# Silu by tanh, the norms' reciprocal root as a power on GpSimd: one ScalarE table per layer

## The chip, the cores and the metric

The kernel runs on one core of a Trainium2 chip. The metric is device time in microseconds. The profile is one execution of the program, taken by the hardware profiler. Engines in it: PE is TensorE, PEld its weight loads, DVE is VectorE, ACT is ScalarE, POOL is GpSimd, SP is SyncE, which here only issues DMAs.

## What is computed

Two layers of the same frame over x of 32 sequences of 256 rows of 128, that is 8192 rows:

```python
xn = _layernorm(x)                       # (x - mean) / sqrt(var + eps)
x = x + attn0(xn) * silu(ffn0(xn))       # layer 0
xn = _layernorm(x)
x = x + attn1(xn) * silu(ffn1(xn))       # layer 1
```

`attn0` is a causal attention of 16 heads of 8 whose pattern is a product of two score matrices, without a softmax. `ffn0` is a mixture of eight experts with gelu and two experts to a row, plus a shared expert; its output is divided by the largest absolute value of its row. `attn1` is a softmax attention over a strided and local set of keys. `ffn1` is a mixture of eight experts with relu, two to a row and a fixed capacity.

## The kernel before

The unit of work is a pair of sequences: `TT` = 4 tiles of 128 rows, so there are `NP` = 16 pairs. In the order of time:

- `begin` (L286), for each pair: `layernorm` (L116), a transpose and the router's product. Beside it the first steps of layer 0's attention run. `route0` (L303) then picks two experts for each row and gives each row a slot.
- Rows are scattered to their slots in device memory by indirect DMAs on POOL (L158), while the attention goes on; then the experts run (`experts`, L572), fetching weights and rows, with some attention steps between.
- The combine of layer 0, `combine0` (L614), for each pair, beside the rest of the attention. It gathers eight tiles of expert rows by indirect DMAs on POOL (L623, into `rows`, four buffers), sums them with their gates on DVE (L632), takes the row's maximum (L636 to L638), applies silu on ACT (L641), multiplies by the attention's output on POOL (L642), adds to x on DVE (L643), writes x back, and takes layer 1's norm (L646), whose result PE transposes for the next router (L650).
- Layer 1: `route1`, a first half of the attention (pairs 0 to 7) while POOL scatters rows, the experts with all weights resident (L1001 to L1044), then the second half of the attention (pairs 8 to 15) beside `combine` (L1050), which gathers expert rows (L1055), sums them with their gates (L1067, L1068), applies silu (L1070), multiplies (L1073), adds (L1074) and stores.

Layer 0's attention handles a sequence in 8 steps. A step transposes features (`ptr`, L440), copies them out of PSUM on ACT (`qk`, L442), makes four pattern matmuls (`pp`, L457) and multiplies them by the causal mask on DVE (`pat`, L459). There are 256 of these products in the run, so they count the attention's progress. Layer 1's attention works in stacks of 128 queries: scores (L831, L838), row maximum and difference on DVE (L846, L847), exponential on ACT (L848), transposes on PE (L853), a copy on ACT (L855), the product with the values (L862).

`layernorm` takes mean and variance on DVE (L121, L122), the root of the variance plus eps on ACT (L124), its reciprocal on DVE (L126), the shift `lnnb` on DVE (L128), and scales four tiles on ACT (L130).

Three things set the order. Each engine works off its own queue in order, so an instruction that waits holds what stands behind it. The order within the queues is made by a scheduler when the program is built, from the order in which the generators above are stepped; PE's order in layer 1's attention is fixed by hand. The generators are stepped by two plans. In layer 0 a pair is started every six attention steps, and its six parts follow at these offsets:

```python
EVERY, LATER = 6, (0, 6, 7, 8, 11, 13)
t0 = at
plan = sorted((t0 + EVERY * p + d, p, n) for p in range(NP) for n, d in enumerate(LATER))
```

In layer 1 the three parts of `combine` come at stacks 2, 5, 6 of every four for the later pairs and 0, 3, 3 for the earlier ones (L1082 to L1087). And the helper `pace` (L138) lets indirect DMAs go three at a time: after every third, a small memset (`breath`, L142) on POOL waits until the three have landed.

ACT evaluates its functions from tables. In the profile a table load (ACT_TABLE_LOAD) stands in front of an activation whose table is not the one that was loaded last: in front of Sqrt, Silu, Gelu, Exp and Sigmoid when the function before was another of these. No load stands in front of copies or of Identity.

Of the kernel before, what the change touches and what calls it, by code (L numbers as in the profile page):

```python
# [11 lines left out]
F32 = mybir.dt.float32  # L12
BF16 = mybir.dt.bfloat16
I32 = mybir.dt.int32
AF = mybir.ActivationFunctionType
ALU = mybir.AluOpType
# [4 lines left out]
P = 128  # L21
# [8 lines left out]
TT = PT // P  # L30
# [5 lines left out]
EPS = 1e-5  # L36
# [6 lines left out]
def bc(ap, axis, n):  # L43

    ap = ap.unsqueeze(axis)
    shape = list(ap.shape)
    shape[axis] = n
    return ap.to_broadcast(shape)
# [8 lines left out]
def model_kernel(ctx: ExitStack, tc: tile.TileContext, a: dict, out: bass.AP):  # L57
    nc = tc.nc
# [12 lines left out]
    const = ctx.enter_context(tc.tile_pool(name="const", bufs=1))  # L71
# [13 lines left out]
    make_identity(nc, ident)  # L85
    identb = const.tile([P, P], BF16, name="identb")
    nc.vector.tensor_copy(identb, ident)
    eps = const.tile([P, 1], F32, name="eps")
    nc.gpsimd.memset(eps, EPS)
    riota = const.tile([P, E], F32, name="riota")  # L90
    nc.gpsimd.iota(riota, [[-1, E]], base=E, channel_multiplier=0,
                   allow_small_or_imprecise_dtypes=True)
# [23 lines left out]
    def layernorm(pool, src, dst, n):  # L116

        st = pool.tile([P, n, 6], F32, tag="lnst", name="lnst")
        mv = pool.tile([P, n, 2], F32, tag="lnmv", name="lnmv")
        for i in range(n):  # L120
            nc.vector.bn_stats(st[:, i, :], src[:, i, :])  # L121
            nc.vector.bn_aggr(mv[:, i, :], st[:, i, :])  # L122
        sd = pool.tile([P, n], F32, tag="lnsd", name="lnsd")
        nc.scalar.activation(sd, mv[:, :, 1], AF.Sqrt, bias=eps)  # L124
        rs = pool.tile([P, n], F32, tag="lnrs", name="lnrs")
        nc.vector.reciprocal(rs, sd)  # L126
        nb = pool.tile([P, n], F32, tag="lnnb", name="lnnb")
        nc.vector.scalar_tensor_tensor(nb, mv[:, :, 0], -1.0, rs, ALU.mult, ALU.mult)  # L128
        for i in range(n):
            nc.scalar.activation(dst[:, i, :], src[:, i, :], AF.Identity, bias=nb[:, i : i + 1],  # L130
                                 scale=rs[:, i : i + 1])
# [89 lines left out]
    with ExitStack() as c0:  # L221
# [26 lines left out]
        def load(p):  # L248
            x = wk.tile([P, TT, P], F32, tag="x", name="x", bufs=6)
            nc.sync.dma_start(x, xin[:, p * TT : (p + 1) * TT, :])  # L250
            return x
# [31 lines left out]
        def mm_tile(name):  # L283
            return ps_m.tile([P, 512], F32, tag="mm", name=name)
# [329 lines left out]
        def combine0(p):  # L614

            t = slice(p * TT, (p + 1) * TT)
            x = load(p)
            so = bk.tile([P, 2, TT, P], F32, tag="soin", name="soin")
            nc.sync.dma_start(so, part[p])
            rows = bk.tile([P, 2, TT, P], F32, tag="rows", name="rows")  # L620
            for i in range(TT):
                for k in range(2):
                    pace(lambda: nc.gpsimd.indirect_dma_start(  # L623
                        out=rows[:, k, i, :], out_offset=None, in_=moe0[:, :],
                        in_offset=bass.IndirectOffsetOnAxis(
                            ap=slot0[:, k, p * TT + i : p * TT + i + 1], axis=0),
                    ))
            yield
            acc = so[:, 1]
            for i in range(TT):  # L630
                for k in range(2):
                    nc.vector.scalar_tensor_tensor(acc[:, i, :], rows[:, k, i, :],  # L632
                                                   gate0[:, k, p * TT + i : p * TT + i + 1],
                                                   acc[:, i, :], ALU.mult, ALU.add)
            mx = wk.tile([P, TT], F32, tag="mx", name="mx")
            nc.vector.tensor_reduce(mx, acc, AX.X, ALU.max, apply_absolute_value=True)  # L636
            nc.vector.tensor_scalar(mx, mx, 1e-6, None, ALU.add)
            nc.vector.reciprocal(mx, mx)  # L638
            yield
            for i in range(TT):  # L640
                nc.scalar.activation(acc[:, i, :], acc[:, i, :], AF.Silu, scale=mx[:, i : i + 1])  # L641
            nc.gpsimd.tensor_tensor(acc, acc, so[:, 0], ALU.mult)  # L642
            nc.vector.tensor_tensor(x, x, acc, ALU.add)  # L643
            nc.sync.dma_start(x1[p], x)
            yield
            layernorm(wk, x, xn[:, t, :], TT)  # L646
            yield
            pst1 = mm_tile("pst1")
            for i in range(TT):
                nc.tensor.transpose(pst1[:, i * P : (i + 1) * P], xn[:, p * TT + i, :], ident)  # L650
            xnT1 = wk.tile([P, PT], F32, tag="xnT1", name="xnT1")
            nc.scalar.copy(xnT1, pst1)
            yield
            psl = mm_tile("psl")
            pl = psl[:, : TT * E].rearrange("p (i e) -> p i e", e=E)
            for i in range(TT):
                nc.tensor.matmul(pl[:, i, :], lhsT=xnT1[:, i * P : (i + 1) * P], rhs=wg1,
                                 start=True, stop=True)
            nc.vector.tensor_copy(logit[:, t, :], pl)
            yield  # L660
# [65 lines left out]
        while plan or at < NP * SPP:  # L726
# [7 lines left out]
            while plan and plan[0][0] < now and plan[0][1] <= (now - 4) // SPP - 1:  # L734
                _, p, n = plan.pop(0)
# [194 lines left out]
    def route1(pool):  # L930
        with ExitStack() as cr:
            rp = cr.enter_context(tc.tile_pool(name="rp", bufs=1))
            NK2 = 2 * NT
            (m0, r0, oh0), (_, r1, oh1) = top2(rp, logit, NT)
            rs = rp.tile([P, 2, NT], F32, name="rs")
            for k, r in enumerate((r0, r1)):
                nc.vector.tensor_copy(rs[:, k, :], r)
            ohf, _, pos = counted(rp, pool, "h", oh0, oh1)
            own = rp.tile([P, E, NK2], F32, name="own")
            for i in range(2):  # L940
                nc.vector.tensor_tensor(own[:, 4 * i : 4 * i + 4, :], pos[i][:, :, :NK2],
                                        ohf[:, 4 * i : 4 * i + 4, :], ALU.mult)
            loc = rp.tile([P, 2, NT], F32, name="loc")
            locf = loc.rearrange("p k n -> p (k n)")
            nc.vector.tensor_reduce(locf, own.rearrange("p e n -> p n e"), AX.X, ALU.add)

            valid = rp.tile([P, 2, NT], F32, name="valid")
            nc.vector.tensor_scalar(valid, loc, float(CAP), None, ALU.is_le)

            slot = rp.tile([P, 2, NT], F32, name="slot")  # L950
            nc.vector.tensor_scalar(slot, rs, -float(CAP), float(E * CAP - 1), ALU.mult, ALU.add)
            nc.vector.tensor_scalar(loc, loc, float(CAP), None, ALU.min)
            nc.vector.tensor_tensor(slot, slot, loc, ALU.add)
            nc.vector.tensor_copy(gidx, slot)
            drop = rp.tile([P, 2, NT], F32, name="drop")
            nc.vector.tensor_scalar(drop, valid, -SKIP, SKIP, ALU.mult, ALU.add)
            nc.vector.tensor_tensor(slot, slot, drop, ALU.add)
            nc.vector.tensor_copy(sidx, slot)  # L958


            ex = rp.tile([P, NT, E], F32, name="ex")
            nc.vector.tensor_tensor(ex, logit, bc(m0, 2, E), ALU.subtract)
            nc.scalar.activation(ex, ex, AF.Exp)
            z = rp.tile([P, NT], F32, name="z")
            nc.vector.tensor_reduce(z, ex, AX.X, ALU.add)
            nc.vector.reciprocal(z, z)
            nc.vector.tensor_tensor(ex, ex, bc(z, 2, E), ALU.mult)
            for k, oh in enumerate((oh0, oh1)):
                nc.vector.tensor_tensor(oh, oh, ex, ALU.mult)
                nc.vector.tensor_reduce(gate[:, k, :], oh, AX.X, ALU.add)  # L970
            nc.vector.tensor_tensor(z, gate[:, 0, :], gate[:, 1, :], ALU.add)
            nc.vector.reciprocal(z, z)
            nc.vector.tensor_tensor(gate, gate, bc(z, 1, 2), ALU.mult)
            nc.vector.tensor_tensor(gate, gate, valid, ALU.mult)

# [21 lines left out]
    with ExitStack() as cm:  # L997
# [35 lines left out]
        rows = [(e, e * CAP + q * MT) for e in range(E) for q in range(CAP // MT)]  # L1033
# [13 lines left out]
    with ExitStack() as cb:  # L1047
        bk = cb.enter_context(tc.tile_pool(name="bk", bufs=3))

        def combine(p):  # L1050

            rows = bk.tile([P, 2, TT, P], F32, tag="rows", name="rows")
# [11 lines left out]
            y = bk.tile([P, TT, P], F32, tag="yc", name="yc")  # L1064
            for i in range(TT):
                n = p * TT + i
                nc.vector.tensor_scalar(y[:, i, :], rows[:, 0, i, :], gate[:, 0, n : n + 1], None, ALU.mult)  # L1067
                nc.vector.scalar_tensor_tensor(y[:, i, :], rows[:, 1, i, :], gate[:, 1, n : n + 1],  # L1068
                                               y[:, i, :], ALU.mult, ALU.add)
            nc.scalar.activation(y, y, AF.Silu)  # L1070
            yield
            s = att.late[p] if p >= NEARLY else sres[:, p * TT : (p + 1) * TT, :]
            nc.vector.tensor_tensor(y, y, s, ALU.mult)  # L1073
            nc.vector.tensor_tensor(y, y, x, ALU.add)  # L1074
            nc.sync.dma_start(outv[:, p * TT : (p + 1) * TT, :], y)
# [122 lines left out]
```

## Time and profile before

| what | value |
|---|---|
| three runs | 2206.1, 2211.04, 2212.84 us; median 2211.04 us |
| profiled execution | 2215.44 us, of which the span is 2213.7 us |
| granted TensorE clock, mean of the span | 0.928 of full speed |
| DVE, waiting for POOL at L643 | 90.5 us, 11 times |
| table loads on ACT | 86, each 1.283 us |
| POOL product L642, 128x512 | 16, mean 1.329 us |
| POOL tensor_tensor L422, 128x1024 | 16, mean 1.954 us |
| DVE 128x512 products (L643, L1073, L1074) | mean 0.66 to 0.69 us |
| silu L641, 128x128 with a scale per row | 64, mean 0.401 us |
| silu L1070, 128x512 | 16, mean 0.630 us |
| root L124, 128x4 | 32, mean 0.301 us |

Stages by the timeline: first norms and routing to about 180 us, scatter to 450, experts to 850, combine of layer 0 with the rest of its attention to 1258, routing and first attention of layer 1 to 1573, its experts to 1819, second attention and combine to the end.

How the page is read: a row of groups gives line, engine, operation, what is written and read, shapes, count, then busy time and the mean in ns of one, then the idle time of the engine just before them and who ended it. A row of waits says which engine at which line waited for whom, how long in total, how often, and the longest. A row of the timeline starts with the start and the length in us; in brackets stands the idle time of the engine before it and what ended it. The clock row and the granted clock say how fast TensorE was allowed to run.

### The profile page before, as it was taken

To read this page: it belongs to the slowest core of one execution; us is meant where nothing else is said; L and a number is where in the kernel's file an instruction comes from. 1 tells how busy PE (TensorE), PEld (TensorE's weight loads), DVE (VectorE), ACT (ScalarE), POOL (GpSimd) and SP (SyncE) were. 2 spreads that over 40 slices of the span, in tenths; PEclk is the share of its full clock that TensorE was granted. 3 is DMA by queue.
4 is the path that set the end of the run, shared out by engine and by line. 5 is a ranking of instruction groups with operands and counts; after the bars stand their busy time and mean duration, and the time that the engine had idled before them with its cause. 6 is when DMAs were issued, how large, how long until landed. Compare 5 with 4: busy or idle time off the path is not lost.

```text
span 2213.7 us, 45584 instructions
## 1 busy us (share of the span) xinstructions
PE 1963.4 (89%) x18674; PEld 1445.9 (65%) x18674; DVE 1232.4 (56%) x2609; ACT 968.0 (44%) x1977; POOL 662.9 (30%) x817
## 2 busy tenths in 40 slices
PE   6999999799999998765969589999999995789898
PEld 4777677588888886544747466666677773456565
DVE  5666766432222224554768477777433335677776
ACT  5623333233334433434746346566311114565655
POOL 0004555413223222555530045543000004444300
PEclk9989999899999999877979789999999997788889
DMA  8702111145545443222220311110122211212100
GB/s 256 215 1 68 52 45 35 57 123 156 156 147 174 147 149 110 77 80 67 82 69 35 110 32 35 38 34 23 53 69 71 72 61 52 52 49 62 44 25 11
DMA packets 131457, 176.80 MB, mean 80 GB/s; under 512 B 16305, under 2 KB 94660, under 8 KB 131249
## 3 DMA queue, kind: packets, MB, share of 16 engines
q1 hardware_dynamic: 103056, 96.57, 13.6%
q0 software_dynamic: 26752, 76.03, 11.7%
q8 instruction: 148, 2.42, 0.5%
q10 hardware_dynamic: 1440, 1.27, 0.2%
q14 instruction: 61, 0.49, 0.1%
HBM read 104.78 MB, written 69.21 MB: 79 GB/s over the span
## 4 chain that ended last, share of the span: by engine, by line
PE 40%; DMA 5%; POOL 4%; ACT 3%; issue 3%; DVE 1%; POOLq 0%; ACTq 0%; DVEq 0%; SPq 0%
PE apsT L853 6%; PE apav L862 6%; PE mpsd L1027 5%; PE mpsu L1014 5%; PE apsc L838 3%; DMA rows<-moe,slot 3%; PE apsc L831 3%; POOL rows L623 2%; DMA rows<-moe,gidx 2%; PE apsf L873 1%; PE apsv L815 1%; ACT apr L848 1%; PE apsk L803 1%; POOL rows L1055 1%; PE pp L457 1%
## 5 line engine op out<-in xcount | busy, mean ns | idle before, releaser
L457 PE MATMUL pp<-qk 64*128 64x128 f32 x2048 | 209.7, 308 | 105.7 <-DVE pat L459 55.5
L442 ACT COPY qk<-ptr 128x512 f32<-128x512 f32 x256 | 149.1, 585 | 353.0 <-PE y L469 270.4
L457 PEld LDWEIGHTS pp<-qk 64*128 64x128 f32 x2048 | 148.0, 192 | 177.2 <-issue 129.8
L459 DVE TENSOR_TENSOR pat<-pp,dmask 128x512 f32<-128x512 f32 x256 | 175.2, 684 | 129.3 <-PE pp L457 128.4
L855 ACT COPY apT<-apsT 124x512 f32<-124x512 f32 x256 | 146.9, 585 | 217.9 <-PE apsT L853 216.6
L1055 POOL DMA_INDIRECT rows<-moe,gidx x128 | 124.5, 973 | 338.8 <-ACT aqT L800 286.5
L862 PEld LDWEIGHTS apav<-ava,apT 124*64 124x64 f32 x4096 | 143.6, 140 | 113.5 <-issue 52.9
L158 POOL DMA_INDIRECT disp<-xn,slot x128 | 136.4, 1066 | 222.4 <-DVE state L432 173.0
L846 DVE TENSOR_REDUCE amx<-apsc 128x4 f32<-128x496 f32 x256 | 159.8, 665 | 75.3 <-PE apsc L838 74.8
L853 PE MATMUL apsT<-ident,apr 128*124 128x128 f32 x1024 | 170.5, 301 | 29.4 <-ACT apT L855 14.6
L608 DVE TENSOR_TENSOR od<-edn,wt 128x256 f32<-128x256 f32 x72 | 30.5, 424 | 287.5 <-PE edn L604 287.5
L862 PE MATMUL apav<-ava,apT 124*64 124x9 f32 x4096 | 167.0, 208 | 22.8 <-ACT apT L855 21.7
L597 ACT ACTIVATE ha<-eup,wt 128x256 f32<-128x256 f32 x288 | 119.0, 470 | 129.7 <-PE eup L592 126.8
L440 PE MATMUL ptr<-ident,feat 128*128 128x128 f32 x1024 | 171.5, 286 | 0.9 <-DVE feat L422 0.6
L848 ACT ACTIVATE apr<-apr 128x496 f32<-128x496 f32 x256 | 149.5, 618 | 30.0 <-DVE apr L847 29.8
L847 DVE TENSOR_TENSOR apr<-apsc,amx 128x496 f32<-128x496 f32 x256 | 159.1, 662 | 0.0
L563 POOL DMA_INDIRECT wt<-in_wexp,wrow x72 | 69.0, 959 | 297.0 <-DVE xdT L585 264.2
L623 POOL DMA_INDIRECT rows<-moe,slot x128 | 133.0, 1039 | 65.6 <-issue 29.0
L853 PEld LDWEIGHTS apsT<-ident,apr 128*124 128x124 f32 x1024 | 120.3, 149 | 47.5 <-ACT apT L855 19.7
L158 POOL DMA_INDIRECT disp<-xn,sidx x128 | 125.8, 983 | 80.5 <-DVE sidx L958 27.1
L440 PEld LDWEIGHTS ptr<-ident,feat 128*128 128x128 f32 x1024 | 120.7, 146 | 43.4 <-issue 38.0
L592 PE MATMUL eup<-xdT,wt 128*128 128x256 f32 x576 | 142.3, 389 | 1.8 <-DMA wt<-in_wexp,wrow 1.8
(217 smaller groups left out, 3671.6 us busy)
## 6 DMA issues: line engine op xcount, KB each, us to landing
disp<-zero SPq DMA_DIRECT2D x17, 1024.0 KB, 6.9
xd<-disp SPq DMA_DIRECT2D x72, 128.0 KB, 2.0
moe<-od SPq DMA_DIRECT2D x72, 128.0 KB, 2.0
x<-in_x SPq DMA_DIRECT2D x32, 256.0 KB, 3.2
part<-so SPq DMA_DIRECT2D x16, 512.0 KB, 3.1
soin<-part SPq DMA_DIRECT2D x16, 512.0 KB, 3.7
xd<-disp SPq DMA_DIRECT2D x32, 256.0 KB, 2.6
moe<-od SPq DMA_DIRECT2D x32, 256.0 KB, 2.0
```

The costliest lines, as they stand in the source:

```text
L158: ins = pace(lambda: nc.gpsimd.indirect_dma_start(out=self.dst[:, :], out_offset=bass.IndirectOffsetOnAxis(ap=idx, axis=0), in_=rows, in_o ...
L440: nc.tensor.transpose(pst[:, 2 * n + c], seq.feat[c][:, n, m * P : (m + 1) * P], ident)
L442: nc.scalar.copy(qk, pst)
L457: nc.tensor.matmul(psp[:, w, c], lhsT=qk[r, 2 + c], rhs=qk[r, c], start=True, stop=True)
L459: nc.vector.tensor_tensor(pat, psp, bc(bc(dmask, 1, 2), 1, 2), ALU.mult)
L623: pace(lambda: nc.gpsimd.indirect_dma_start(out=rows[:, k, i, :], out_offset=None, in_=moe0[:, :], in_offset=bass.IndirectOffsetOnAxis(ap= ...
L846: nc.vector.tensor_reduce(mx, sv, AX.X, ALU.max)
L847: nc.vector.tensor_tensor(to, sv, bc(mx, 2, NK), ALU.subtract)
L848: nc.scalar.activation(to, to, AF.Exp)
L853: nc.tensor.transpose(psT[:NK, j, :], pr[:, 4 * g + j, :], ident)
L855: nc.scalar.copy(pT[:NK], psT[:NK])
L862: nc.tensor.matmul(avv[u * QB : (u + 1) * QB, h, :], lhsT=pT[:NK, j, u * QB : (u + 1) * QB], rhs=va[:NK, 2 * st + u, h, :], start=True, st ...
```

## The change

Three edits, in both layers:

- `layernorm`: instead of a root on ACT and a reciprocal on DVE, DVE adds eps and POOL raises the sum to the power -0.5, by a tensor_tensor with a constant tile `minus`. A norm now asks ACT for Identity alone. It holds for all 32 norms.
- `combine0`: silu(v) is written as v/2 * (1 + tanh(v/2)). DVE halves the reciprocal maximum and scales the whole pair by it (one 128x512 product in place of the scale in four activations). ACT takes one tanh of 128x512, written into `rows[:, 0]`. The product with the attention's output moves from POOL to DVE (it goes into `so[:, 0]`), and a scalar_tensor_tensor on DVE forms (th + 1) times that.
- `combine`: the half is put into the gates (one small multiplication in `route1`), ACT takes tanh into `rows[:, 0]`, and DVE forms (th + 1) * y before the product with the attention's output.

In the built program tanh stands behind gelu in layer 0, and beside exponentials in layer 1, without a table load between them; the program has 6 table loads.

```diff
-    eps = const.tile([P, 1], F32, name="eps")
-    nc.gpsimd.memset(eps, EPS)
+    minus = const.tile([P, TT], F32, name="minus")
+    nc.gpsimd.memset(minus, -0.5)
...
-        sd = pool.tile([P, n], F32, tag="lnsd", name="lnsd")
-        nc.scalar.activation(sd, mv[:, :, 1], AF.Sqrt, bias=eps)
         rs = pool.tile([P, n], F32, tag="lnrs", name="lnrs")
-        nc.vector.reciprocal(rs, sd)
+        nc.vector.tensor_scalar(rs, mv[:, :, 1], EPS, None, ALU.add)
+        nc.gpsimd.tensor_tensor(rs, rs, minus[:, :n], ALU.pow)
...
             nc.vector.reciprocal(mx, mx)
-            yield
-            for i in range(TT):
-                nc.scalar.activation(acc[:, i, :], acc[:, i, :], AF.Silu, scale=mx[:, i : i + 1])
-            nc.gpsimd.tensor_tensor(acc, acc, so[:, 0], ALU.mult)
+            nc.vector.tensor_scalar(mx, mx, 0.5, None, ALU.mult)
+
+            nc.vector.tensor_tensor(acc, acc, bc(mx, 2, P), ALU.mult)
+            th = rows[:, 0]
+            nc.scalar.activation(th, acc, AF.Tanh)
+            yield
+            nc.vector.tensor_tensor(so[:, 0], so[:, 0], acc, ALU.mult)
+            nc.vector.scalar_tensor_tensor(acc, th, 1.0, so[:, 0], ALU.add, ALU.mult)
             nc.vector.tensor_tensor(x, x, acc, ALU.add)
...
             nc.vector.reciprocal(z, z)
+
+            nc.vector.tensor_scalar(z, z, 0.5, None, ALU.mult)
             nc.vector.tensor_tensor(gate, gate, bc(z, 1, 2), ALU.mult)
...
-            nc.scalar.activation(y, y, AF.Silu)
+            th = rows[:, 0]
+            nc.scalar.activation(th, y, AF.Tanh)
             yield
             s = att.late[p] if p >= NEARLY else sres[:, p * TT : (p + 1) * TT, :]
+            nc.vector.scalar_tensor_tensor(y, th, 1.0, y, ALU.add, ALU.mult)
             nc.vector.tensor_tensor(y, y, s, ALU.mult)
```

## The prediction

> **What bounds the kernel now.** The page first: busy shares, and TensorE over the 40 slices.
>
> ```profile
> span 2213.7 us, 45584 instructions
> PE 1963.4 (89%) x18674; PEld 1445.9 (65%) x18674; DVE 1232.4 (56%) x2609; ACT 968.0 (44%) x1977; POOL 662.9 (30%) x817
> ...
> PE   6999999799999998765969589999999995789898
> ```
>
> PE is the bound at 9 and makes way to something else at 5 to 8: slices 15 to 23 (layer 0's combine beside the rest of its attention, 855 to 1258 us) and from slice 33 (layer 1's second attention beside its combine). ACT, from which the change takes most, is busy 44%: its time counts only where it is waited for. So next the table loads, from the groups of ACT by form (count, busy us, mean ns, idle before):
>
> ```profile
> L486 ACT ACT_TABLE_LOAD x18 | 23.1, 1283 | 0.3
> L641 ACT ACT_TABLE_LOAD x18 | 23.1, 1283 | 9.7 <-DVE mx L638 9.5
> L124 ACT ACT_TABLE_LOAD x17 | 21.8, 1283 | 9.5 <-DVE lnmv L122 9.2
> L1070 ACT ACT_TABLE_LOAD x15 | 19.2, 1283 | 0.3
> L848 ACT ACT_TABLE_LOAD x15 | 19.2, 1283 | 0.3
> ```
>
> By the timeline, of 86 loads 11 lie before 180 us, 44 in the combine of layer 0, 30 in that of layer 1. Then the waits in layer 0's combine (850 to 1126 us), and its longest hole in the timeline:
>
> ```profile
> DVE x L643 <- POOL soin L642: 84.4, 8, 24.9
> POOL breath L142 <- DMA rows<-moe,slot: 71.5, 38, 5.2
> PE pp L457 <- DVE pat L459: 31.4, 5, 12.5
> ...
> 1118.48 0.94 POOL L623 DMA_INDIRECT rows<-moe,slot  x1 [0.27 <-POOL breath L142]
> 1119.45 1.27 POOL L642 TENSOR_TENSOR soin<-soin 128x512 f32<-128x512 f32 x1
> 1120.75 0.69 DVE L643 TENSOR_TENSOR x<-x,soin 128x512 f32<-128x512 f32 x1 [20.47 <-POOL soin L642]
> 1125.49 0.68 DVE L459 TENSOR_TENSOR pat<-pp,dmask 128x512 f32<-128x512 f32 x1
> 1126.32 1.22 PE L457 MATMUL pp<-qk 64*128 64x128 f32 x8 [20.90 <-DVE pat L459]
> ```
>
> The silu was ready long before; its product sat on POOL behind gathers that leave three at a time. DVE stood 20.47 us at its sum, the pattern product behind it stood too, and PE 20.90 us. Not ACT but the POOL queue bounds this stage. Layer 1, steady part:
>
> ```profile
> 2097.06 1.28 ACT L848 ACT_TABLE_LOAD   x1
> 2098.35 1.12 ACT L848 ACTIVATE apr<-apr 128x496 f32<-128x496 f32 x2
> 2099.38 0.56 ACT L855 COPY apT<-apsT 124x512 f32<-124x512 f32 x1
> 2100.00 0.64 PE L862 MATMUL apav<-ava,apT 124*64 124x9 f32 x16 [1.69 <-ACT apT L855]
> ```
>
> Here a load is on the chain: load, exponential, copy, PE. Behind it PE runs slow for some 5 us (apsT, eight transposes: 1.96 us at 2104, 1.04 in an unhindered stack); the granted clock over 1895 to 2150 us is 0.83, in the same attention without a combine (1290 to 1573 us) 0.99.
>
> **The change, part by part.** The order of the built programs shows 6 loads where there were 86, so ACT loses 80 x 1.283 = 103 us. The Trainium skill (ScalarE: Activation LUTs, What ACT_TABLE_LOAD costs) adds a drain of about 1.38 us to each switch; by that it would be 213 us. The rows contradict it: 0.3 us idle before 15 loads, and at 2098.35 the exponential starts 0.01 us after its load. I count 1.283.
>
> Before 180 us: PE is busy 99.66 of 100 us from 50 to 150, so the 6 loads that go there lie under PE. At the start DVE waits for a small DMA until 13.15 us before its first scale, which also covers the first powers. The 16 powers of the first norms run on a POOL idle from 4.6 to 178 us; if that cover were gone, each would cost its own length. I take 0, at most 3 either way. The extra halving in the routing of layer 1 is one 0.2 us operation.
>
> Layer 0's combine, 16 pairs. POOL loses a product (16 x 1.33 us) and gains a power; ACT loses 44 loads, four silus of 0.40 and a root of 0.30 per pair, and gains a tanh of 0.63 (by the 128x512 silu row of L1070); DVE gains three 128x512 operations of 0.69 and one of 0.17, 2.2 us a pair, while the reciprocal is replaced by an addition of the same size. From 855 to 1126 us DVE is busy 153.3 of 271, and 85.9 of 114 after that: it can hide 2.2 us per pair, but not much more.
>
> What matters is the queue. In the order of the changed program the power of a pair stands on POOL behind a gather, and the shift `lnnb` that waits for it stands on DVE before further pattern products, as the sum stood before. So the wait is moved, not removed. The positions of the first twelve powers: behind gathers 22, 37, 52, 61, 70, 76, 85, 93, 100, 108, 116, 124, with DVE at pattern product 172, 179, 185, 190, 196, 203, 209, 214, 220, 227, 233, 238 of 256. Before, the products stood behind gathers 18, 28, 43, 58, 59, 88, 98, 100, 122, 124 and the sums at 171, 176, 181, 187, 190, 199, 206, 208, 218, 218. The long jumps (29 and 22 gathers for 9 and 10 products) are gone, the small ones are more even. A second tie is new: tanh is written into `rows`, so the gather of the pair four later waits until DVE has used it: gather 49 for product 183, 57 for 189, 65 for 194, 73 for 201 and so on to 121 for 237; behind such a gather wait the others and the next power.
>
> Price of each step from the trace: three gathers take 5.8 us (3 x 0.94 issued, 2 x 0.30 between, 1.7 to the landing, 0.7 for the breath); 30 pattern products between 1150 and 1240 us, 3.0 us each with all that goes beside them, and 1.5 us for PE's slow restart after a hole (5, 6, 9 and 10 products between holes took 17, 20.6, 29.3 and 28.3 us). The power itself shows nowhere in the trace. Low end 0.13 us (IOTA of 128x8); near it lies POOL's product: 1.33 us at 512 wide and 1.95 at 1024 leave 0.7 at 4 wide. The skill speaks against it: GPSIMD Engine Reference, Instruction dispatch, tells of 5.95 us for the first call of a kernel just loaded; if every power between two DMAs paid that, it would be 6. But L642 alternates with gathers in the same way and takes 1.27 us. I take 1.0, nearest to L642's fixed part; high end 6.
>
> Walking both queues, taking the later at each meeting: the first power is done at 907 us (gather 22 went at 906 already), the next at 939 (15 gathers, 29 us, and 1; DVE would be there at 930), 969 (DVE 958), 992, 1016. From there a pair is a round: 4 or 5 products from the meeting to the use of tanh (13.5 to 16.5 us), then 4 to 6 gathers in the queue (7 to 8 us) and the power, about 23.5 us for some 6 products: 1041, 1064, 1086, 1108, 1132, 1153, 1174. Then 18 products without gathers, 55.5 us: the 256th at 1230 instead of 1240 us. After it the tail of the last pair loses two loads and POOL's product and gains DVE's work: -1. Gain 11 us; each microsecond of power adds 12.
>
> Layer 1's combine. Until about 1903 us gathers bound it (rows of the first five pairs arrive every 15.6 us: eight gathers), and that stays. From 1906 to 2142 us 22 stacks take 236 us; undisturbed in the first attention they take 8.96 us each, 197 in all. The excess of 39 us is the 23 loads (29.5 us), the combine's own work and the slow clock. The loads go. New is a scalar_tensor_tensor of 0.69 on DVE, which in the new order stands directly behind the last operation of `y` and so waits for tanh: 0.63 and two hand-overs, some 0.85 us in which the row maxima behind it wait. DVE is busy 189 of 255 us, 15.9 per two stacks; with 1.5 more 17.4, PE needs 17.9. I take 19.2 per two stacks with one combine, 1.3 over PE alone: 11 x 19.2 = 211, a gain of 25 us. Bounds: nothing if DVE's new wait makes PE pause as the load did, 35 if all but DVE's work goes.
>
> Sum: -11 - 25 = -36. The profiled execution took 2215.4 us (span 2213.7 and 1.7 around it) and would come to 2179; against the median of the runs, 2211.0, it is 2175.
>
> **The rivals.** DVE becomes the bound: if its 2.2 us a pair (0.37 a product) do not fit beside the pattern products, the some 65 products on the path of layer 0 take 24 us more, and that stage ends 13 us late: 2199. For it: DVE is busy 79 to 88% between the holes even now. Against it: PE was 97% busy after 1126 us with DVE at 75%.
>
> The tie is looser: if DVE and PE catch up between short holes, as 10 products in 28.3 us suggest, the stage nears its floor, 855 + 93 x 3.0 = 1134 us and some 35 for the worst meetings, 1170 instead of 1240: about 60 more, 2115 to 2120. Against it: no stretch with gathers ran so.
>
> Slower: the power's price. At 12 on the path it eats the gain from 1 + 36/12 = 4.0 us; at 6 us it is 60 more, 2235, DVE waiting at each `lnnb` with the pattern products behind it. Against it: L642's 1.27 us. For it: no POOL instruction of this trace evaluates a power.
>
> That the tables do not fall away is excluded by the built order; that their fall is worth its 103 us is against the 44% of ACT.
>
> **How the numbers follow.** 0.46 for the forecast (2155 to 2200), 0.20 for DVE as bound (2199, of which 0.08 within 0.3%), 0.20 for the looser tie, 0.14 for a dear power (above 2217). About 0.3%, 6.6 us, is what a measurement tells from no change. Faster 0.76 = 0.44 + 0.12 + 0.20, same 0.10 = 0.02 + 0.08, slower 0.14. The range 2120 to 2222 leaves out the far part of the third and most of the fourth.
>
> **What would show it.** 6 table loads; the power's row on POOL near 1 us and 16 of 32 among gathers; DVE waiting for POOL at `lnnb` 8 to 12 times, 50 to 65 us in all instead of 90.5 over the whole run; gathers waiting for the use of tanh; the 256th pattern product near 1230 us; 9.6 us a stack after 1900 us with a clock of 0.9 or more. I am wrong if the power is above 4 us, if the gathers no longer meet DVE, or if the stacks stay at 10.7 us.

## The result

The changed kernel takes 2202.77 us in the median of 14 runs, the kernel before 2212.38 us on the same chip: ratio 0.9958, 95% interval 0.9942 to 0.9974. It is faster, by 0.4% and not by the 1.6% of the forecast. The profiled execution took 2200.98 us, span 2199.2.

The runs were made on several chips, and on two of them (kernel before at 2280 and 2266 us) layer 1's first attention takes 48 to 60 us longer in every profile, at a granted clock of 0.86 to 0.90 instead of 1.00, so ratios are always to the kernel before on the same chip, and stages are compared by their own length.

### The profile page after: what moved, and what is told of

It is laid out like the page before. It is cut to its first block, busy times and chain, and to the rows that moved or that the text cites. A ratio compares the mean times of both kernels' runs of the same rounds, so it can differ in the third digit from the quotient of the medians.

```text
span 2199.2 us, 45580 instructions
## 1 busy us (share of the span) xinstructions
PE 1988.7 (90%) x18674; PEld 1455.2 (66%) x18674; DVE 1267.9 (58%) x2690; ACT 852.9 (39%) x1817; POOL 672.4 (31%) x833
## 5 line engine op out<-in xcount | busy, mean ns | idle before, releaser
L456 PE MATMUL pp<-qk 64*128 64x128 f32 x2048 | 216.2, 314 | 40.0 <-ACT qk L441 17.0
L439 PE MATMUL ptr<-ident,feat 128*128 128x128 f32 x1024 | 176.7, 291 | 1.6 <-ACT qk L441 1.1
L856 PEld LDWEIGHTS apsT<-ident,apr 128*124 128x124 f32 x1024 | 115.6, 146 | 53.8 <-ACT apT L858 30.3
```

The costliest lines, as they stand in the source:

```text
L439: nc.tensor.transpose(pst[:, 2 * n + c], seq.feat[c][:, n, m * P : (m + 1) * P], ident)
L456: nc.tensor.matmul(psp[:, w, c], lhsT=qk[r, 2 + c], rhs=qk[r, c], start=True, stop=True)
L856: nc.tensor.transpose(psT[:NK, j, :], pr[:, 4 * g + j, :], ident)
```

## The profile after

The page: span, busy shares, and PE and its granted clock over the 40 slices.

```profile
span 2199.2 us, 45580 instructions
PE 1988.7 (90%) x18674; PEld 1455.2 (66%) x18674; DVE 1267.9 (58%) x2690; ACT 852.9 (39%) x1817; POOL 672.4 (31%) x833
...
PE   6999999799999998678889869999899996699998
...
PEclk9999999899999999887889969999999998689989
```

ACT is 115 us less busy (968.0 before), and the kernel did not follow. PE is 25 us busier than before (1963.4) for the same instructions: that is the line to stop at. In slices 15 to 22 (counted from 0), layer 0's combine, PE now shows 6 to 9 almost evenly, where before it fell to 5 in two slices.

The groups of ACT and POOL that the change made:

```profile
L129 ACT ACT_TABLE_LOAD x1 | 1.3, 1283 | 9.2 <-DMA wout<-in_wout 9.2
L705 ACT ACT_TABLE_LOAD x1 | 1.3, 1283 | 0.0
L351 ACT ACT_TABLE_LOAD x1 | 1.3, 1283 | 0.0
L966 ACT ACT_TABLE_LOAD x1 | 1.3, 1283 | 0.0
...
L125 POOL TENSOR_TENSOR lnrs<-lnrs,minus 128x4 f32<-128x4 f32 x32 | 34.6, 1082 | 109.3 <-DVE lnrs L124 103.9 <-DVE lnmv L122 5.2
```

With two more at L485 there are 6 loads. The power takes 1.08 us in the mean (1.01 to 1.06 in 29 of 32). Both as forecast.

The waits in layer 0's combine (850 to 1280 us; of the engine and line named first, for the one named second: us in all, how often, the longest):

```profile
ACT xn L129 <- DVE lnnb L127: 88.2, 16, 14.1
POOL rows L622 <- DVE soin L645: 72.3, 8, 18.9
DVE lnnb L127 <- POOL lnrs L125: 71.5, 16, 9.5
...
PE pst L653 <- ACT xn L129: 56.0, 12, 12.9
```

Before, DVE waited 90.5 us in 11 waits for the product, the longest 24.9 (at L643). Now it waits 71.5 us for the power, in 16 waits of at most 9.5. The chain goes on: ACT's scale waits for the shift, PE's transposes of the norm (`pst`) for the scale, and the gathers for the use of tanh. One meeting in the timeline (the gathers that came first, the power, then shift, scale, transposes):

```profile
1010.90 0.95 POOL L622 DMA_INDIRECT rows<-moe,slot  x1 [0.30 <-issue]
1012.16 0.95 POOL L622 DMA_INDIRECT rows<-moe,slot  x1 [0.30 <-issue]
1013.13 1.04 POOL L125 TENSOR_TENSOR lnrs<-lnrs,minus 128x4 f32<-128x4 f32 x1
1014.21 0.16 DVE L127 SCALAR_TENSOR_TENSOR lnnb<-lnmv,lnrs 128x4 f32<-128x4 f32 x1 [6.62 <-POOL lnrs L125]
1014.41 1.65 ACT L129 ACTIVATE xn<-x,lnnb,lnrs 128x128 f32<-128x128 f32 x4 [8.91 <-DVE lnnb L127]
1014.96 1.63 PE L653 MATMUL pst<-ident,xn 128*128 128x128 f32 x4 [5.07 <-ACT xn L129]
...
1018.18 1.22 PE L456 MATMUL pp<-qk 64*128 64x128 f32 x8
...
1036.94 0.71 PE L456 MATMUL pp<-qk 64*128 64x128 f32 x8
```

PE stood 5.07 us. Three microseconds after the hole eight pattern matmuls take 1.22 us, 22 microseconds after it 0.71. The table by stretches (its length, PE's busy time, the granted clock) says why:

```profile
core 0: us, PE busy (x), PEclk, DMA share, GB/s
1015.00:1032.00 17.00, 16.98 (x88) 0.50 0.09 24
1036.00:1043.00 7.00, 7.00 (x76) 1.00 0.39 128
```

For 17 us PE is busy almost without a gap, at half its clock. The busy share hides this entirely.

The stages, from the two profiles. "Combine 0" runs from the start of the first gather to that of the 256th pattern product on DVE. A stack of layer 1's attention is taken at the transpose of its output on PE (`apso`, L868 before), so "half b" runs from the end of the second attention's first stack to the end of the program. "Half clock" is what the record of the clock shows at 0.5.

| stage, us | before | after |
|---|---|---|
| start to the first gather | 855.2 | 855.2 |
| combine 0 | 378.5 | 394.0 |
| on to the last stack of the first attention | 338.2 | 338.6 |
| on to the first stack of half b | 298.5 | 297.0 |
| half b | 343.3 | 314.4 |
| combine 0: PE busy, then idle | 292, 87 | 329, 66 |
| combine 0: stretches at half clock, their length, PE busy in them | 7, 95.6, 36.5 | 14, 109.2, 88.3 |

Layer 1 gained 29 us; layer 0's combine lost 15.5 of it. There PE's idle time fell by 21 us, as it should, but the same work took PE 37 us more. In place of 7 holes (stretches in which PE stands idle) of 2.7 to 22.8 us there are 13 of 2.0 to 8.1 us, and behind each of them PE works on at half clock (the 14th stretch, at 1124 us, stands behind no idle time over 0.8 us). Before, 59 of the 95.6 us at half clock lay inside the holes, where they cost nothing.

## The experiments

Combine 0 and half b from one profile of each run, with each run's ratio to the kernel before on its chip (A is the chip of the first result; layer 1's first attention is slow on B). The changed kernel itself was run on A and C alone. One profile tells combine 0 to some 6 us, between chips to 12: the same layer 0 took 388.0 to 394.0 us in four profiles (two of them of the calm runs below), and norm on DVE 320.9 and 308.7.

| run | chip | combine 0 | half b | ratio (95%) |
|---|---|---|---|---|
| before | A | 378.5 | 343.3 | 1 |
| changed | A | 394.0 | 314.4 | 0.9958 (0.9942 to 0.9974) |
| changed, again | C | 388.0 | 316.2 | 0.9956 (0.9942 to 0.9970) |
| layer 1 alone | B | 370.8 | 341.3 | 0.9930 (0.9906 to 0.9954) |
| layer 0 alone | B | 395.3 | 354.1 | 1.0096 (1.0068 to 1.0123) |
| norm on DVE | B | 320.9 | 340.0 | 0.9703 (0.9649 to 0.9757) |
| tanh in its own tile | B | 385.2 | 347.8 | 1.0014 (0.9986 to 1.0042) |
| root on ACT | C | 304.5 | 308.9 | 0.9541 (0.9518 to 0.9564) |
| product on DVE | C | 310.8 | 344.9 | 0.9717 (0.9694 to 0.9740) |
| power twice | C | 408.7 | 321.4 | 1.0041 (1.0025 to 1.0058) |
| silu and power | D | 383.9 | 315.2 | 0.9919 (0.9903 to 0.9936) |
| filled holes | D | 456.9 | 311.0 | 1.0225 (1.0208 to 1.0243) |
| norm on DVE, second | D | 308.7 | 316.3 | 0.9601 (0.9582 to 0.9619) |
| root on ACT, own tile | D | 306.1 | 308.2 | 0.9526 (0.9511 to 0.9542) |

### The two layers apart

Layer 1 alone: the kernel before with these lines.

```diff
+            nc.vector.tensor_scalar(z, z, 0.5, None, ALU.mult)
...
-            nc.scalar.activation(y, y, AF.Silu)
+            th = rows[:, 0]
+            nc.scalar.activation(th, y, AF.Tanh)
...
+            nc.vector.scalar_tensor_tensor(y, th, 1.0, y, ALU.add, ALU.mult)
```

> Layer 1's part of the change alone: tanh and the halved gate there, layer 0's silu and all norms as before. Theory (the two layers' effects simply add, as the stage ends of the changed kernel's profile say: layer 0's combine +15.5 us, layer 1's second attention with its combine -29.6): 256th pattern product at 1234 us as before, span about 2184, 2182 us in the median, ratio 0.987. Rival (the gain in layer 1 comes from the changed start, since the changed kernel enters that stage 14 us later with the same gathers): the stage keeps its 321 us less a few, span 2205 or more. The first exponential of layer 1 still finds another table loaded, so about 57 loads.

Measured: 0.993, combine 0 370.8 us, 56 table loads. Faster, but by 0.7% where 1.3% were expected. Layer 0 alone is the changed kernel with these lines taken back:

> Layer 0's part alone: power on GpSimd for the norms, tanh, product on VectorE; layer 1's combine keeps its silu. Theory (effects add): 256th pattern product at 1249 us, span about 2229, ratio 1.006 to 1.008: this half of the change makes the kernel slower. Rival (what is lost in layer 0 is paid only because of something in layer 1): span at or below 2214.

Measured: 1.0096, combine 0 395.3 us. So the direction holds: layer 0's half of the change makes the kernel slower, layer 1's makes it faster. Their sum is not tested well, because this chip gives back less in half b: 354.1 minus 341.3 is 13 us, against 29 on chip A.

### Which of the ties in layer 0 costs

The root by two Newton steps on VectorE, so that no norm passes through GpSimd:

```diff
-        nc.vector.tensor_scalar(rs, mv[:, :, 1], EPS, None, ALU.add)
-        nc.gpsimd.tensor_tensor(rs, rs, minus[:, :n], ALU.pow)
...
+        nc.vector.tensor_scalar(va, mv[:, :, 1], EPS, None, ALU.add)
+        nc.vector.tensor_scalar(rs, va, 1.0, 0.5, ALU.add, ALU.mult)
+        nc.vector.reciprocal(rs, rs)
...
+        for _ in range(2):
+            nc.vector.tensor_tensor(tn, rs, rs, ALU.mult)
+            nc.vector.scalar_tensor_tensor(tn, tn, -0.5, va, ALU.mult, ALU.mult)
+            nc.vector.scalar_tensor_tensor(rs, tn, 1.5, rs, ALU.add, ALU.mult)
```

> The changed kernel with the reciprocal root taken on VectorE by two Newton steps (nine 128x4 operations in place of one; it holds for variances near one), so that no norm goes through GpSimd. Theory A (the power behind the gathers holds VectorE at the shift, PE waits behind it for the norm's transposes, and each of the some 14 short holes brings a slow-clock restart): the holes go, 256th pattern product near 1165 us (93 products of 3.0 us from 855 and about 1 us a pair for the small operations, and the first gathers' wait), granted clock of the stage 0.95 or more, span about 2115 to 2130, ratio 0.96. Theory B (VectorE is simply full with its 2.2 us more a pair): the small operations add to it, 256th product at 1255 or later, span 2200 to 2215. Theory C (the tie of the gathers to tanh's tile is what paces the stage, VectorE's wait for the power only follows it): the gathers wait as before for the use of tanh, 72 us, 256th product within 10 us of 1249.

Measured: ratio 0.9703, 256th product at 1175.5 us, combine 0 320.9 us. The stage answers much as theory A said (1165), though VectorE got more work, so B falls. The tie through tanh's tile is still there, but the gathers wait for VectorE 1.2 us in all instead of 72, so C falls. The whole time, 2212, is not the 2115 to 2130 expected, because of the chip: it is 68 us under the kernel before there.

Tanh in a tile of its own:

```diff
-            th = rows[:, 0]
+            th = wk.tile([P, TT, P], F32, tag="th", name="th")
```

> The changed kernel with tanh written into a tile of its own, so that a gather no longer waits for the use of tanh four pairs before; the power stays on GpSimd, behind 22, 37, 54, 64, 72, 79, 88, 96, 104, 112, 120 and 128 gathers. Theory A (it is a loop of two ties: power behind gathers, gathers behind tanh's use; either cut opens it): gathers run on at 1.95 us each, the last power among them near 1120 instead of 1197 us, VectorE stops waiting at the shift from about the sixth pair, 256th product near 1183 us, span 2135 to 2150, ratio 0.965 to 0.975. Theory B (VectorE full): no change, 2195 to 2205. Theory D (only the power's place counts, the tie of the gathers is slack): 256th product within 10 us of 1249, gathers waiting for other things instead.

Measured: 1.0014, combine 0 385.2 us, 256th product at 1244.6 us. My claim that either cut opens the loop is wrong, and D holds for the stage. (The changed kernel was not run on this chip, so the ratio has no partner.) The waits for the power and of the gathers in this run:

```profile
DVE lnnb L127 <- POOL lnrs L125: 60.4, 15, 12.6
POOL rows L622 <- DVE soin L631: 47.4, 7, 15.1
```

They now wait for L631, which reads the gathered rows of four pairs earlier: with four buffers this tie was always there, mostly two or three pattern products ahead of tanh's use, and the scheduler put the powers behind two to four gathers more. VectorE still waits 60 us for the power.

### Without GpSimd, with the table loads

Root on ACT: the changed kernel with the norms of before.

```diff
-        nc.vector.tensor_scalar(rs, mv[:, :, 1], EPS, None, ALU.add)
-        nc.gpsimd.tensor_tensor(rs, rs, minus[:, :n], ALU.pow)
...
+        nc.scalar.activation(sd, mv[:, :, 1], AF.Sqrt, bias=eps)
+        nc.vector.reciprocal(rs, sd)
```

First the changed kernel itself, once more, as the measure of this chip:

> The changed kernel once more, beside the next three on one chip, as their common measure. Stage times as in its first profile where TensorE's clock is alike: 256th pattern product 394 us after the first gather of layer 0's combine. Theory: ratio to the kernel before 0.994 to 1.000; on a chip whose clock is granted less in layer 1's attention the gain of layer 1 is smaller (13 us there instead of 29 between the two half-changes), so nearer to 1.000.

Measured: 0.9956, as the first time; combine 0 388.0, half b 316.2 us. Then the root on ACT:

> The changed kernel with the norms as before: root on ScalarE, reciprocal on VectorE; silu by tanh and the product on VectorE stay. No GpSimd operation stands between the gathers, but root and gelu or tanh now change tables (some 47 loads in all instead of 6). Theory A (the power's place among the gathers is what costs): although table loads come back, the 256th product comes about 325 us after the first gather (1180 us if that starts at 855) instead of 394, and the kernel is 60 to 70 us faster than the changed one. Theory B (VectorE full): 385 us or more. Theory E (ScalarE's loads on the norm's path cost as much as the power): 375 us or more.

Measured: 2101.50 us in the median, ratio 0.9541, combine 0 304.5 us with 47 table loads. That is 95 us under the changed kernel beside it; of the 98 between the two profiles 84 lie in combine 0. Theory A, and more than it asked; B and E fall. The page and the waits of this run:

```profile
span 2096.5 us, 45610 instructions
PE 1947.4 (93%) x18674; PEld 1429.6 (68%) x18674; DVE 1265.7 (60%) x2690; ACT 912.8 (44%) x1890; POOL 644.6 (31%) x801
...
PE   6999999969999999899999599999999996799998
```

```profile
POOL breath L142 <- DMA rows<-moe,slot: 82.7, 41, 4.4
...
POOL rows L623 <- issue: 29.6, 82, 3.1
POOL rows L623 <- POOL breath L142: 20.1, 39, 0.6
```

Between its gathers GpSimd now waits for its own transfers, and no wait of VectorE for GpSimd is left. The same table by stretches, of this kernel over its combine 0, of the changed one over its own, and of the kernel before:

```profile
core 0: us, PE busy (x) PEld busy (x) DVE busy (x) ACT busy (x) POOL busy (x), PEclk, DMA share, GB/s
849.00:1154.00 305.00, 291.72 (x2939) 208.38 (x2936) 261.06 (x641) 169.07 (x326) 140.49 (x171) 0.98 0.26 85
```

```profile
855.00:1250.00 395.00, 328.77 (x2948) 231.66 (x2944) 264.20 (x644) 124.17 (x280) 150.41 (x186) 0.86 0.22 66
```

```profile
855.00:1234.00 379.00, 291.58 (x2933) 211.28 (x2934) 237.71 (x583) 189.70 (x384) 157.22 (x186) 0.87 0.22 68
```

DVE has the same work in the first two (261 and 264 us busy); PE needs 292 us at clock 0.98 and 329 at 0.86. The mean clock alone does not tell this: the kernel before has 0.87 and 292 us, for its slow clock lay mostly in its holes. ACT, with its loads back, is 45 us busier (169 against 124), and no cost of it shows in the stage.

Product on DVE: the kernel before with one word changed.

```diff
-            nc.gpsimd.tensor_tensor(acc, acc, so[:, 0], ALU.mult)
+            nc.vector.tensor_tensor(acc, acc, so[:, 0], ALU.mult)
```

> The kernel before with one word changed: the product of silu and attention in layer 0 on VectorE instead of GpSimd. All silus, roots and all 86-odd table loads stay. Theory A: the stage opens as with the root on ScalarE, 256th product 325 to 335 us after the first gather (before: 378), 45 to 50 us faster than before, which would put this word alone far ahead of the whole change. Theory E (ScalarE's loads bound the stage once GpSimd is out): 360 us or more. Theory B (VectorE full): within 10 us of 378.

Measured: 0.9717, combine 0 310.8 us (325 to 335 expected), with 92 table loads. One word is worth 66 us, the whole change beside it 10. In layer 0 the tanh form, which has 15 loads fewer in the stage and three more 128x512 operations a pair on VectorE, is worth 6 us net (310.8 against 304.5), no more than that scatter. In layer 1, where 27 loads fall from half b and one operation a pair is added, it is worth 36 (344.9 against 308.9).

Power twice:

```diff
...
-        nc.gpsimd.tensor_tensor(rs, rs, minus[:, :n], ALU.pow)
+        nc.gpsimd.tensor_tensor(rs, rs, less[:, :n], ALU.pow)
+        nc.gpsimd.tensor_tensor(rs, rs, half[:, :n], ALU.pow)
```

> The changed kernel with the power in two, first to -1 and then to 0.5, one directly behind the other on GpSimd in all but a few places (a gather between them in four). Each norm costs one power more, some 1.03 us. Theory A (a power stands on the round of each pair, 12 among gathers): 256th product 12 to 16 us later than in the changed kernel beside it, ratio to it 1.006 to 1.007. Theory B or D (the power is hidden behind VectorE's own work): less than 4 us.

Measured: 20.7 us more in combine 0 than the changed kernel beside it, ratio between the two medians 2215.14 / 2196.78 = 1.0084, 18 us. The power lies on the path, and 1.03 us more of it cost about one and a half times the 12 us per us of my sum.

Silu and power: the changed kernel with layer 0's silu of before, its product on GpSimd.

```diff
...
-            nc.vector.tensor_tensor(so[:, 0], so[:, 0], acc, ALU.mult)
-            nc.vector.scalar_tensor_tensor(acc, th, 1.0, so[:, 0], ALU.add, ALU.mult)
...
+            nc.gpsimd.tensor_tensor(acc, acc, so[:, 0], ALU.mult)
```

> The changed kernel with layer 0's silu as before (four silus on ScalarE, product on GpSimd); the norms' power stays on GpSimd, layer 1 as changed. It is the fourth corner of a square: first gather to 256th product 378 us with product on GpSimd and root on ScalarE, 304 with both off GpSimd, 388 to 394 with the power alone on it. Theory A (each operation among the gathers is a meeting of the two queues): with both, two meetings a pair, 395 to 430 us. Rival F (once VectorE waits for the product, the power behind it has been done meanwhile and costs nothing): 378 within 8.

Measured: 383.9 us. Here theory A's reading (two operations, two meetings) falls, and rival F holds: one operation among the gathers costs 68 us (product: 378.5 against 310.8, chips A and C) to 84 us (power: 388.0 against 304.5, both on C) over none, a second one nothing that shows (383.9).

```profile
DVE lnnb L127 <- POOL lnrs L125: 44.3, 14, 9.4
DVE x L642 <- POOL soin L641: 43.2, 11, 14.0
```

VectorE waits 44 and 43 us for the two, 88 in all, about what it waited for the one product before (90.5). So the two waits share what one operation cost alone: it is the place in the queue that is waited for.

Two more on the form without GpSimd, beside one another on one chip:

> The root by Newton steps on VectorE again, now on the chip of the next one, to compare the two ways of keeping the norm off GpSimd. Theory A with VectorE at 85% busy once the queues are apart: its eight small operations more a pair lie on the path, some 1 us a pair, so the stage takes 318 to 323 us against 304 with the root on ScalarE, and the kernel 12 to 18 us more than that one, although it has 6 table loads and that one 47. Rival (loads on ScalarE cost more than the small operations): this one is the faster.

Measured: combine 0 308.7 us, 4 more than with the root on ACT. The same program took 320.9 on chip B, so my price of 1 us a pair for the small operations is not settled: 4 to 16 us in all. The kernel is 16 us slower than the next one all the same (2120.19 against 2104.02); of the 11.6 us between the two profiles 8 lie in half b, where both run the same program. Why it runs slower there is open.

> Root on ScalarE, silu by tanh, product on VectorE, and tanh in a tile of its own: no tie is left but the four buffers of the gathered rows. Theory A (with no GpSimd operation among the gathers, the wait of the gathers for tanh's use hides): stage within 5 us of the 304 of the root on ScalarE with tanh in rows, time within 0.3% of it (ratio to the kernel before 0.951 to 0.957). Theory C (the tie through the rows' tile still costs): 8 us or more faster.

Measured: ratio 0.9526, not to be told from 0.9541; combine 0 306.1 us. Once no GpSimd operation stands among the gathers, the tie through tanh's tile costs nothing that shows.

### The price of a hole

Filled holes: work for PE in front of the norm's transposes.

```diff
             pst1 = mm_tile("pst1")
+            if p < 12:
+                for _ in range(7):
+                    nc.tensor.matmul(pst1, lhsT=ident, rhs=upw, start=True, stop=True)
```

> The changed kernel with seven matmuls of 128x512 (some 0.5 us each at full clock, 3.5 us together) put on PE directly in front of the norm's transposes of the first twelve pairs; they go into the same PSUM tile, which the transposes then overwrite, so they add only work. PE has them to do while the power and the shift are on their way. Theory A1 (each short hole ends in a restart of PE at half clock, some 3 us: 80 to 88 us of the stage PE works at half clock): the half-clock time in which PE is busy falls under 40 us, and although PE gets 42 us of work more, the stage from first gather to 256th product becomes shorter than the changed kernel's 388 to 394 us: 365 to 380. Rival A2 (the restart is not what costs; the wait for the power alone sets the round): the stage stays within 5 us or grows by up to 40. The order of the powers among the gathers moves a little (behind 22, 37, 48, 61, 67, 80, 82, 91, 98, 108, 117, 127), which could make 5 us either way.

Measured: 456.9 us, 63 more than the changed kernel. It settles nothing. The added matmuls took 76 us in all, not 42 (84 of them show as 168 records of 606 ns in the mean), longer than the holes, and the scheduler, which knew of them, put the last power among the gathers at pattern product 209 instead of 238, so that 47 products were left for the end. Half-clock time with PE busy was 64.5 us: less than 88.3, more than the 40 expected.

So the price was measured where nothing else moves, in layer 1's experts, which PE does without a gap at full clock. In every second of 32 blocks a copy on VectorE that PE needs is written several times over:

```diff
-            nc.vector.tensor_copy(xdT, pst[:, :MT])
+            for _ in range(17 if row // MT % 2 else 1):
+                nc.vector.tensor_copy(xdT, pst[:, :MT])
```

The short form has 9 in place of 17.

> The changed kernel with one copy of layer 1's experts (their transposed rows, PSUM to SBUF on VectorE) written nine times over instead of once in every second of the 32 blocks; nothing computed changes. That stage is PE-bound and calm (clock 1.00, PE busy 209.9 of 210 us in the changed kernel), and layer 0's order stays as it was. PE finds some 2 us of hole in each of 16 blocks, some 15 us apart. Theory A1 (what my sum lacked is the half clock after a hole): holes this short bring little or no half-clock time, the stage grows by PE's idle time and not by more than 10 us beyond it. Rival A2 (PE's extra busy time in layer 0's combine has nothing to do with holes): PE's busy time is unchanged in both runs.

Measured: one run on another chip (E). One hole of 0.9 us in 242.2 us, and PE busy 241.3. VectorE's slack was larger than I had counted. It serves as the zero of the next.

> The same with seventeen copies: holes of 6 to 7 us in 16 blocks. Theory A1: after each hole PE works some 3.4 to 7 us at half clock, so its busy time in the stage grows by 1.7 to 3.5 us a hole, 27 to 56 us in all, on top of the idle time; the granted clock in the records falls to about 0.7 to 0.8. Rival A2: PE's busy time stays as it is, the stage grows by the idle time alone.

Measured, in one run beside the short form: the stage takes 356.2 us (by PE's first and last instruction in it) instead of 242.2. PE is idle 75.9 us, in 16 holes of 4.6 to 6.7 us, and busy 280.3 instead of 241.3: 2.4 us more a hole, in the middle of the 1.7 to 3.5 expected; the granted clock over the stage is 0.88, higher than I had put. A2 falls. The clock record has a stretch at half speed for each of the 16 holes, of 3.4 or 6.8 us, starting 2.5 to 5.0 us after PE stopped; PE is busy for 75 us at half clock (5 in the short form), and half of the difference, 35 us, is most of the 39 us of more busy time. The timeline of one (in the changed kernel eight of these matmuls take 3.60 us, so 16 take 7.2), and the granted clock over the hole's last microsecond and the 4 us behind it, then further on:

```profile
1723.05 8.83 PE L1020 MATMUL mpsu<-xdT,w 128*128 128x512 f32 x16 [4.57 <-DVE xdT L1015]
1731.72 3.73 PE L1033 MATMUL mpsd<-w,hd 128*128 128x128 f32 x32
```

```profile
core 0: us, PE busy (x), PEclk, DMA share, GB/s
1722.00:1726.70 4.70, 3.65 (x5) 0.64 0.00 0
1726.70:1738.00 11.30, 11.30 (x69) 1.00 0.09 16
```

## Why the prediction was wrong

Right in kind: what bounds the stage, and what the change does to it. The 6 loads, the power's price (1.0 taken, 1.05 among the gathers), the ends of the first five powers (907, 939, 969, 992, 1016 forecast; 904, 936, 966, 990, 1014 measured), the gathers' wait for tanh's use, the wait that is moved and not removed. That wait was larger than forecast, 71.5 us in 16 waits against 50 to 65 in 8 to 12.

**Layer 1: right in kind, and in size by luck.** Forecast a gain of 25 us, 236 to 211; the same stretch, 1906.3 to 2142.4 before, takes 211.6 us. But I called it 22 stacks, and between its ends lie 21. So a stack took 11.2 us before and 10.1 after, not 10.7 and 9.6: with the right count my 9.6 would have promised 202 us and a gain of 35. The count and the price were wrong by the same share, and the two errors cancelled. The stacks around it gave 4 us more. Over half b PE's idle time fell 18 us and its busy time 11; its half-clock time when busy fell from 87 to 62 us, half of which, 13 us, covers those 11. So the slow clock that I had only noted was over a third of the gain.

**Layer 0: wrong, +15.5 us in place of -11.** Two terms failed.

The first is a reading: "the 256th at 1230 instead of 1240". The 256th product of the kernel before starts at 1233.7; 1240 was the end of a window. On its own figures the walk promised 4 us, not 10. That is 6 us of the 26 that were missed.

The second is the step "1.5 us for PE's slow restart after a hole", and with it the round of 23.5 us. From the fifth power to the twelfth I had 158 us (22.6 a round, by the times listed); measured are 184.4, 26.3 a round. Split at the use of tanh: from a power to it 119.7 us for 30 products, where 30 x 3.0 + 7 x 1.5 = 100.5 were counted; from it through the gathers to the end of the next power 64.4, where 7 x 8.5 = 59.5 were (both together 160, 2 more than the times listed). So 19 of the 24 to 26 us lie in PE's own leg. In these 184 us PE works 58.0 us at half clock, which costs 29.0, 4.1 a round where I had 1.5: 18.5 us, most of the 24 to 26. Some 4 us more may be the price of a product, an estimate: where PE has hardly a hole (root on ACT) it is busy 3.13 us a product, not 3.0, and there are 30. I took the 1.5 us from four stretches of the kernel before, whose few long holes had their slow clock mostly inside the hole; at 3.0 us a product these leave 2.0, 2.6, 2.3 and -1.7 us. The Trainium skill (TensorE: Matmul & The Clock Gate, What's actually happening) has the rule that I left aside: the clock halves after about 3.4 us idle and comes back after about 3.4 us of work. By it a hole costs 1.7 us, an estimate from that figure. The trace is dearer: stretches of 3.4, 6.8, 10.2 and once 17.1 us, the last with PE busy throughout, and holes of 2.0 to 2.6 us brought one too. So it is 4.1 us a round in this stage and 2.4 a hole in the calm one.

**The rivals.** "DVE becomes the bound" gave 2199, close to the measured time, and is wrong: with the same VectorE work and no GpSimd operation the stage takes 304.5 us. That a rival's number fits is no evidence for its mechanism. "The looser tie" (1170 for the 256th) is about what happens when the GpSimd operation goes: 1154 to 1176 us. "The dear power" did not occur.

Shown is: an operation on GpSimd among the gathers costs 66 us or more (product, whole kernel on chip C), whichever it is, and the change swapped one for another. Shown is, too, the half clock behind short holes, in the stage and apart from it, and that PE's busy time goes with it: over 15 profiles with the same PE work in combine 0 (all but the filled holes), PE's busy time without the norm's transposes rises by 0.42 us for each us worked at half clock, from 276 us with 8 to 309 with 90 (correlation 0.99). Argued only: that the 37 us of more PE time are 26 of half clock (half of 88.3 - 36.5) and 10 in which the record of the norm's transposes (19.8 us against 9.4) stretches over its waits; the run that should have removed the holes alone did not do so.

## What to carry to other kernels

Where a queue issues paced gathers, look first for the operation on it that another engine waits for, even one of 1 us, and move that one, before counting table loads on an engine that is 44% busy. When a wait is cut up, count the holes as well as their sum: in the calm stage a hole of some 4.7 us cost PE 2.4 us more afterwards, in the combine a round cost 4.1 us, and the busy share shows that as work. Best here is the form without GpSimd in the combine: root on ScalarE, tanh, product on VectorE, 0.954 of the kernel before.

## What the runs showed that was not expected

- Busy time is no measure of PE's work: 292 and 329 us for the same instructions. The sign is the time at half clock in which PE is busy (36.5 and 88.3 us), not the mean clock of the stage (0.87 and 0.86).
- 33 table loads on ScalarE within layer 0's combine change nothing that can be seen there (304.5 us with them, 308.7 with none and the root on VectorE), while in layer 1, where a load stands between exponential and PE, the form without them was worth 29 us (before and changed, chip A) and 36 (product on DVE and root on ACT, chip C), but 13 on chip B.
- Chips differ: on B, layer 1's first attention takes 326 us at clock 0.86 (layer 1 alone) where it takes 266 at 1.00 on A (before), with the same attention code. There, on B, PE has no hole over 1.6 us and still eleven stretches at half clock, of 3.4 to 20.5 us. So a hole is not the only thing that goes before a slow clock, and the records do not say what else does.
